# Two attention layers on one core: other PSUM banks and a split load at the start, and two kinds of VectorE work placed later

## The chip, the cores and the metric

The kernel runs on one core of a Trainium2 chip. A core has five engines that work side by side and wait for each other through semaphores: TensorE (matmuls, PE in the profile, with its weight loads as PEld), VectorE (DVE), ScalarE (ACT), GpSimd (POOL) and SyncE (SP), which issues most of the transfers. Matmuls write to PSUM, and VectorE or ScalarE must copy or add the result out of PSUM before a bank can be written again. The metric is the device time of one execution in microseconds (us). All data is float32.

## What is computed

Eight images of 32x32 positions and 256 channels go through two layers. The first is attention with four heads, an output projection and a residual; the second is attention with 32-channel queries and keys, scaled by gamma, with a residual.

```python
# layer 0; xf: (8, 1024, 256), 4 heads
qkv = einsum('bnc,cd->bnd', xf, W_qkv)             # per head q, k, v of 256 each
atten = softmax(einsum('bihd,bjhd->bijh', q, k) * 256**-0.5, axis=2)
res = einsum('bijh,bjhd->bihd', atten, v)
x = einsum('bnd,dc->bnc', res.reshape(B, -1, 1024), W_out) + b_out + xf
# layer 1
f, g, h = x @ Wf + bf, x @ Wg + bg, x @ Wh + bh     # f, g: 32 wide, h: 256 wide
b = softmax(einsum('bik,bjk->bij', g, f), axis=-1)
y = gamma * einsum('bij,bjd->bid', b, h) + x
```

## The kernel before

Positions are taken in two blocks of 512 (blk 0 and 1), channels in two halves of 128, since a tile has 128 partitions. In layer 0 the weights of a head are multiplied together first (`fold_weights`, lines 302 to 351): Wq with Wk transposed gives `wqk`, and Wv with that head's part of W_out gives `wvo`. For this the three weight blocks are turned by TensorE transposes against an identity (tasks `turn`, PSUM tiles pwq, pwk, pwv), copied to SBUF as wqT and wvT, and multiplied (tasks `multiply`, PSUM tiles pwqk and pwvo). `copy_on(i, dst, src)` puts a copy on VectorE where i is even and on ScalarE where it is odd.

Most products use Strassen's scheme with seven block products in place of eight (`seven`, line 235). Each has three PSUM banks, x, y and z, and is cut into three tasks, one, two and three. Task two ends with VectorE's `v = y + e` and `out22 = z + v`; task three's matmuls then write bank y again, so they wait for v. Operands of the block products are sums and differences of blocks, which VectorE makes beforehand: xs from the transposed image (`key_sums`), qs from the queries, ss from the exponentials of the scores, yt from the products.

PSUM has eight banks. The pool tagged "ps" holds six of them, for the scores and most block products; the pool "psm" holds two, for transposes, weight products and the output projection. Tiles of a pool go round: a new one starts when the reader of the one that many places back has finished.

For the first image the rows are turned by TensorE in `transpose_rows` (line 357, PSUM tiles px, copied to x0T by ScalarE). Later images are turned by small transfers on SP (`turn_rows`, line 401, issued at line 386) and VectorE's 32x32 transpose (line 394). The order at the start is written out (lines 965 to 971): turn q and k of head 0, half of px, multiply wqk, the rest of px, turn v, two of the xs sums, multiply wvo, the other two sums, then the first queries together with head 1's weights.

After that the program goes through steps (line 983 on), one for each head and block of layer 0 and one for each block of layer 1. For images 1 to 7 layer 1 of the image before comes between heads: after two heads, or after all four for the last image. In each step, tasks of several heads in flight are collected with a place on a scale of 0 to 10, and issued in the order of these places, to all engines. Scores of the step stand at 0, 2, 4, 6, 8 and 10 in layer 0; products and projections of the two steps before go between them. Each engine works through its own list in that order, so an instruction that waits holds up everything behind it on its engine.

Two kinds of tasks matter here besides the start.

- The scaling. The row sums of the exponentials are added over the partitions by POOL, go through DRAM to become a column, are inverted by VectorE (line 642), and go back through DRAM as a row that is broadcast to all partitions (`inv` and `invb`, lines 647 and 649, on SP's queue). One step after the projection, VectorE multiplies the projected tile `o` with it (line 700), and POOL issues a transfer that adds o to x1T, layer 1's input (line 703). The lists of these tasks are in `adds`.
- The next image's sums. While head 2 is worked on, the next image is turned, and in block 1 of that head its four xs sums are made (`key_sums`, line 433).

```python
        if i - 1 in adds:
            put(adds[i - 1], 0.5 if l0 or blk == 1 else 2.3)
...
            put(key_sums(a.b + 1), 0.5, 0.6, 6.4, 7.4)
```

Of the kernel before, what the change touches and what calls it, by code (L numbers as in the profile page):

```python
# [16 lines left out]
P = 128  # L17
# [3 lines left out]
def kernel(  # L21
# [52 lines left out]
    nc = tc.nc  # L74
    B, H, W, C = x.shape
# [5 lines left out]
    NB = 512  # L81
# [29 lines left out]
    def tile_of(tag, shape, name):  # L111
        return pools[tag].tile(shape, F32, tag=tag, name=name)


    rows, rows1 = {}, {}
# [57 lines left out]
    def copy_on(i, dst, src):  # L173
        if i % 2 == 0:
            nc.vector.tensor_copy(dst, src)
        else:
            nc.scalar.copy(dst, src)
# [6 lines left out]
    def load_weights(h, tag):  # L184

        nw = CC * 3 * C
        t = tile_of(tag, [P, nw + CC * C], f"w_{h}")
        w = t[:, :nw].rearrange("p (c d) -> p c d", c=CC)
        wo = t[:, nw:].rearrange("p (c d) -> p c d", c=CC)
        weights[h] = w, wo  # L190
        v = wqkv_v[:, :, ts(h, 3 * C)]

        def load_qk():
            nc.sync.dma_start(w[:, :, : 2 * C], v[:, :, : 2 * C])

        def load_v():
            nc.sync.dma_start(w[:, :, 2 * C :], v[:, :, 2 * C :])
            nc.sync.dma_start(wo, wout_v[:, ts(h, CC), :])

        return [load_qk, load_v]  # L200
# [4 lines left out]
    def sum_a(sums, a11, a12, a21, a22):  # L205
        tt = nc.vector.tensor_tensor
        s1, s2, s3, s4 = sums
        return [
            partial(tt, s1, a21, a22, ALU.add),
            partial(tt, s2, s1, a11, ALU.subtract),  # L210
            partial(tt, s3, a11, a21, ALU.subtract),
            partial(tt, s4, a12, s2, ALU.subtract),
        ]

    def sum_b(sums, b11, b12, b21, b22):
        tt = nc.vector.tensor_tensor
        t1, t2, t3, t4 = sums
        return [
            partial(tt, t3, b22, b12, ALU.subtract),
            partial(tt, t1, b12, b11, ALU.subtract),  # L220
            partial(tt, t2, b22, t1, ALU.subtract),
            partial(tt, t4, b21, t2, ALU.subtract),
        ]

    def a_operands(blocks, sums):
        a11, a12, a21, a22 = blocks
        s1, s2, s3, s4 = sums
        return dict(zip((1, 2, 3, 4, 5, 6, 7), (a11, a12, s4, a22, s1, s2, s3)))

    def b_operands(blocks, sums):  # L230
        b11, b12, b21, b22 = blocks
        t1, t2, t3, t4 = sums
        return dict(zip((1, 2, 3, 4, 5, 6, 7), (b11, b21, b22, t4, t1, t2, t3)))
# [65 lines left out]
    NARROW = dict(e="eh", u="uh", v="w")  # L299
    LAST = dict(e="eo", u="uo", v="w")  # L300

    def fold_weights(h):

        wT, hold = [], []
        folded[h] = []

        def turn(i, what):
            w, _ = weights[h]
            pt = tile_of("psm", [P, NB], f"pw{what}_{h}")
            for d in range(CC):  # L310
                for c in range(CC):
                    nc.tensor.transpose(
                        pt[:, d * C + c * P : d * C + (c + 1) * P],
                        w[:, c, i * C + d * P : i * C + (d + 1) * P],
                        ident,
                    )
            if i != 1:
                hold.append(tile_of("y", [P, N], f"w{what}T_{h}"))
            t = hold[-1][:, ts(i % 2, NB)]
            copy_on(i, t, pt)  # L320
            wT.append(t.rearrange("p (d c) -> p d c", d=CC))

        def multiply(i, what):
            pm = tile_of("psm", [P, NB], f"p{what}_{h}")
            for c in range(CC):
                for d in range(CC):
                    nc.tensor.matmul(
                        pm[:, ts(c, C)],
                        lhsT=wT[2 * i][:, d, ts(c, P)],
                        rhs=wT[1][:, d, :] if i == 0 else weights[h][1][:, d, :],  # L330
                        start=(d == 0),
                        stop=(d == CC - 1),
                    )
            t = const.tile([P, CC, C], F32, tag=f"{what}{h}", name=f"{what}{h}")
            copy_on(i, t.rearrange("p c e -> p (c e)"), pm)
            folded[h].append(t)
            if i == 0:
                t4 = const.tile([P, 4, P], F32, tag=f"wt{h}", name=f"wt{h}")
                sums = [t4[:, k, :] for k in range(4)]
                blocks = [t[:, c, ts(e, P)] for c in range(CC) for e in range(CC)]  # L340
                run(sum_b(sums, *blocks))
                wblocks[h] = b_operands(blocks, sums)
            else:
                t4 = const.tile([P, 4, P], F32, tag=f"wo{h}", name=f"wo{h}")
                sums = [t4[:, k, :] for k in range(4)]
                blocks = [t[:, c, ts(e, P)] for e in range(CC) for c in range(CC)]
                run(sum_a(sums, *blocks))
                oblocks[h] = a_operands(blocks, sums)

        tasks = [partial(turn, i, what) for i, what in enumerate(("q", "k", "v"))]  # L350
        tasks += [partial(multiply, i, what) for i, what in enumerate(("wqk", "wvo"))]
        return tasks


    xT_of, x1T_of, xblocks, vblocks = {}, {}, {}, {}

    def transpose_rows(b, src, dst, layer):


        def task(k, c):  # L360
            if b not in dst:
                dst[b] = tile_of("xT", [P, CC, N], f"x{layer}T_{b}")
            pt = tile_of("psm", [P, NB], f"px{layer}_{b}_{k}_{c}")
            for t in range(HT):
                nc.tensor.transpose(
                    pt[:, ts(t, P)], src[b][:, k * HT + t, ts(c, P)], ident
                )
            nc.scalar.copy(dst[b][:, c, ts(k, NB)], pt)

        return [partial(task, k, c) for k in range(NBLK) for c in range(CC)]  # L370
# [50 lines left out]
    def key_sums(b):  # L421

        made = {}

        def piece(i):
            if i == 0:
                xT = xT_of[b]
                t = tile_of("v", [P, 4, HN], f"xs_{b}")
                sums = [t[:, k, :] for k in range(4)]
                blocks = [xT[:, c, ts(k, HN)] for k in range(2) for c in range(CC)]  # L430
                made["l"] = sum_a(sums, *blocks)
                xblocks[b] = a_operands(blocks, sums)
            made["l"][i]()

        return [partial(piece, i) for i in range(4)]
# [479 lines left out]
    def run(*lists):  # L915
        for l in lists:
            for t in l:
                t()
# [27 lines left out]
    pm = tile_of("psm", [P, NB], "pm_idle")  # L946
# [10 lines left out]
    steps, adds = [], {}  # L957
# [6 lines left out]

    first = steps[0][0]
    queries, qsums = first.queries(), first.query_sums(0)
    turn_q, turn_k, turn_v, fold_qk, fold_vo = fold_weights(0)
    turn_x, sums = transpose_rows(0, rows, xT_of, 0), key_sums(0)
    fold = [fold_weights(h) for h in range(1, HEADS)]
    run([turn_q, turn_k], turn_x[:2], [fold_qk], turn_x[2:], [turn_v], sums[:2], [fold_vo])  # L970
    run(sums[2:], queries[:2], fold[0][:2], queries[2:], qsums)
    first_sums = value_sums(0)

    def is_l0(s):
        return s is not None and isinstance(s[0], Layer0)

    def step(k):
        return steps[k] if 0 <= k < len(steps) else None
# [4 lines left out]
    for i, (a, blk) in enumerate(steps):  # L983
        l0 = isinstance(a, Layer0)
        one, two, nxt = step(i - 1), step(i - 2), step(i + 1)
        places = []

        def put(tasks, *at):
            assert len(tasks) == len(at)
            places.extend(zip(at, range(len(places), len(places) + len(at)), tasks))  # L990
# [3 lines left out]
        else:  # L994
            tasks, _ = a.scores(blk)
            put(tasks, *((0.5, 2.4) if blk == 0 else (0.5, 2)))
        if is_l0(two):
            u, k = two
# [9 lines left out]
            if nxt is None:  # L1008
                put(adds[i], 4.2)
        if i - 1 in adds:  # L1010
            put(adds[i - 1], 0.5 if l0 or blk == 1 else 2.3)
        if is_l0(one):
            u, k = one
            sums, keys = u.sums(k)
# [31 lines left out]
        if l0 and a.h == 2 and a.b + 1 < B:  # L1046
            if blk == 0:
                put(moves[4:], 0.5, 1.5, 2.5, 3.5)
                put(turned, 6.4, 7.4, 8.4, 9.4)
            else:  # L1050
                put(key_sums(a.b + 1), 0.5, 0.6, 6.4, 7.4)

        if l0 and a.b > 0 and a.h == behind(a.b) - 1:
            if blk == 0:
# [106 lines left out]
    with tc.If(bad > 0), ExitStack() as general:  # L1161
# [7 lines left out]
        for b in range(B):  # L1169
# [3 lines left out]
            for h in range(HEADS):  # L1173
                a = General0(b, h, bout_sb)
# [4 lines left out]
            a = Layer1(b)  # L1179
# [37 lines left out]
```

## Time and profile before

| | |
|---|---|
| median of three runs | 2309.2 us (2309.19 to 2309.86) |
| profiled execution, whole | 2311.76 us |
| profiled execution, span of the program's instructions | 2309.9 us |
| TensorE granted clock | 1.00 |
| VectorE / ScalarE / POOL busy | 72% / 25% / 14% of the span |
| DMA, mean | 41 GB/s, 94.16 MB |

The span runs from the first instruction to the end of the last one. The profiled execution is a single one, and its own total is set beside its span. In the timeline a line has the start in us, the busy time in us, the engine, the source line, the operation, output and inputs by the program's names with their shapes, and how many instructions were merged; in brackets stands how long the engine was idle before it and who released it. Names without numbers stand for many tiles: psx, psy and psz are the three banks of any block product of the scores, and psy_y, psy_q and psy_o those of products, queries and projections.

### The profile page before, as it was taken

How to read it: one execution, taken by the hardware profiler on the slowest of the kernel's cores; microseconds unless marked ns; L12 is line 12 of the kernel's file. 1: busy time of each engine (PE TensorE's matmuls, PEld its weight loads, DVE VectorE, ACT ScalarE, POOL GpSimd, SP SyncE). 2: the span in 40 equal slices, each digit the busy share in tenths (PEclk: the TensorE clock that was granted, in tenths of full speed). 3: DMA queues.
4: the chain of work that ended last, by engine and by line, in shares of the span. 5: the costliest groups of instructions: out<-in, count | busy, mean ns of one | idle time of the engine just before them, and what ended most of it. 6: DMA issues, size and time to landing. Idle time of an engine off the chain costs nothing.

```text
span 2309.9 us, 27289 instructions
## 1 busy us (share of the span) xinstructions
PE 2299.7 (100%) x10256; PEld 1891.9 (82%) x10256; DVE 1663.3 (72%) x2963; ACT 585.5 (25%) x1015; POOL 317.9 (14%) x199
## 2 busy tenths in 40 slices
PE   9999999999999999999999999999999999999999
PEld 7888888788878888778887888878888788888887
DVE  7787787577875777657776677766777667777765
ACT  2222222222221222212232122221222222222223
POOL 0111112011120112101121011210112101111210
PEclk9999999999999999999999999999999999999999
DMA  4211123301233013220132201322113211121222
GB/s 137 33 28 26 21 38 52 74 15 28 35 52 68 15 28 47 47 61 15 28 55 43 58 15 28 58 42 55 19 23 58 42 37 19 28 45 25 40 45 49
DMA packets 239740, 94.16 MB, mean 41 GB/s; under 512 B 204208, under 2 KB 208944, under 8 KB 239600
## 3 DMA queue, kind: packets, MB, share of 16 engines
q1 hardware_dynamic: 220400, 55.10, 12.3%
q0 software_dynamic: 19200, 37.23, 9.2%
q8 instruction: 83, 1.36, 0.4%
q14 instruction: 57, 0.47, 0.1%
HBM read 29.76 MB, written 8.65 MB: 17 GB/s over the span
## 4 chain that ended last, share of the span: by engine, by line
PE 96%; DMA 3%; DVE 1%; SPq 0%; ACT 0%; issue 0%; DVEq 0%
PE psy_y L255 14%; PE psy L255 14%; PE psx_y L255 10%; PE psz_y L255 10%; PE psz L255 9%; PE psx L255 9%; PE pa_l L900 8%; PE psy_o L255 6%; PE psy_q L255 3%; PE pr_v_l L494 3%; PE psx_q L255 2%; PE psx_o L255 2%; PE psz_q L255 2%; DMA inv<-inverse 2%; PE ps_l L812 1%; DMA invb<-inv 1%
## 5 line engine op out<-in xcount | busy, mean ns | idle before, releaser
L626 POOL PARTITION_ALL_REDUCE rb<-rs x64 | 206.6, 3229 | 1429.2 <-DVE rs L624 901.3
L255 PE MATMUL psx<-q,x0T 128*128 128x256 f32 x1024 | 263.5, 380 | 0.0
L255 PE MATMUL psy<-qs,xs 128*128 128x256 f32 x1024 | 262.9, 379 | 0.0
L255 PE MATMUL psz<-q,xs 128*128 128x256 f32 x1024 | 262.8, 379 | 0.0
L576 ACT ACTIVATE p<-p 128x1024 f32<-128x1024 f32 x128 | 135.3, 1057 | 497.7 <-DVE p L272 497.7
L255 PE MATMUL psx_y<-p,x 128*128 128x256 f32 x1024 | 241.9, 379 | 0.0
L255 PE MATMUL psy_y<-p,xt 128*128 128x256 f32 x1024 | 241.9, 379 | 0.0
L900 PE MATMUL pa_l<-v_l,s_l 128*128 128x257 f32 x1024 | 231.5, 381 | 0.0
L255 PEld LDWEIGHTS psx<-q,x0T 128*128 128x128 f32 x1024 | 193.8, 190 | 45.3 <-issue 20.7
L255 PEld LDWEIGHTS psx_y<-p,x 128*128 128x128 f32 x1024 | 194.6, 190 | 34.1 <-issue 8.6
L900 PEld LDWEIGHTS pa_l<-v_l,s_l 128*128 128x128 f32 x1024 | 193.9, 190 | 32.9 <-issue 6.1
L255 PEld LDWEIGHTS psy<-qs,xs 128*128 128x128 f32 x1024 | 194.5, 190 | 26.8 <-DVE q L272 0.4
L255 PEld LDWEIGHTS psz<-q,xs 128*128 128x128 f32 x1024 | 194.6, 190 | 26.5
L255 PEld LDWEIGHTS psy_y<-p,xt 128*128 128x128 f32 x1024 | 194.6, 190 | 26.5
L284 ACT ACTIVATE p<-psx 128x512 f32<-128x512 f32 x128 | 76.4, 597 | 363.7 <-PE psx L255 363.5
L272 DVE TENSOR_TENSOR u<-psy,e 128x512 f32<-128x512 f32 x128 | 88.1, 689 | 87.0 <-ACT e L278 75.6
L703 POOL DMA_DIRECT2D x1T<-o x64 | 78.0, 1219 | 431.9 <-DVE o L700 303.6
L255 PE MATMUL psy<-qs,x0T 128*128 128x256 f32 x512 | 132.6, 381 | 1.6 <-DVE v L272 1.6
L272 DVE TENSOR_TENSOR v<-psy,e 128x512 f32<-128x512 f32 x128 | 88.3, 690 | 53.0 <-PE psy L255 51.7
L255 PE MATMUL psy_y<-ss,xt 128*128 128x256 f32 x512 | 121.4, 380 | 0.1
L255 PE MATMUL psz_y<-ss,xt 128*128 128x256 f32 x512 | 120.9, 379 | 0.0
L255 PE MATMUL psz_y<-ss,x 128*128 128x256 f32 x512 | 120.9, 379 | 0.0
(141 smaller groups left out, 3419.4 us busy)
## 6 DMA issues: line engine op xcount, KB each, us to landing
x1T<-o POOLq DMA_DIRECT2D x64, 512.0 KB, 5.0
invb<-inv SPq DMA_DIRECT2D x63, 256.0 KB
x<-x1T SPq DMA_DIRECT2D x256, 32.0 KB
out_dram<-x SPq DMA_DIRECT2D x15, 512.0 KB
x<-in_x_dram SPq DMA_DIRECT2D x14, 512.0 KB
x0T<-x SPq DMA_DIRECT2D x224, 32.0 KB
fg<-v_l POOLq DMA_DIRECT2D x56, 64.0 KB, 2.1
w<-in_L_conv_W_qkv_dram SPq DMA_DIRECT2D x4, 512.0 KB
```

Of the source, the lines that this page charges most:

```text
L255: nc.tensor.matmul(banks[k][:, ts(i, w)], lhsT=lhsT, rhs=rhs, start=first and n == 0, stop=True, skip_group_check=True,)
L272: nc.vector.tensor_tensor(dst, shaped(banks[k]), shaped(other), ALU.add)
L284: copy(outs["11"](), shaped(banks["x"]))
L494: nc.tensor.matmul(pm[:, ts(j, C)], lhsT=src()[:, c, ts(2 * t2 + j, P)], rhs=w()[:, c, :], start=(c == 0), stop=(c == CC - 1),)
L576: exp(both, both)
L626: nc.gpsimd.partition_all_reduce(t, r.rearrange("p e i -> p (e i)"), P, bass_isa.ReduceOp.add)
L703: nc.gpsimd.dma_start(x1T_of[self.b][:, :, ts(blk, NB)], o, accum_op=ALU.add)
L812: nc.tensor.matmul(pm, lhsT=self.f[ts(r, CK), ts(j0 + r, P)], rhs=self.g[ts(r, CK), ts(blk, NB)], start=True, stop=True,)
L900: nc.tensor.matmul(pm[:, : C + 1], lhsT=p[:, j, ts(ti, P)], rhs=v[:, j, : C + 1], start=(j == 0), stop=(j == NT - 1),)
```

## The change

- The first load of head 0's weights, q and k in one transfer of 512 KB, becomes two transfers of 256 KB, one for q and one for k. Other heads keep one transfer.
- The transposes and weight products of head 0 and the transposes of the first image's rows take their PSUM tiles from "ps" in place of "psm" (nine tiles).
- In all four heads the copy of the turned v weights (wvT) moves from VectorE to ScalarE: `(i + 1) // 2` is 0 for q, 1 for k and 1 for v. The copies of wqT, wqk, wkT and wvo stay.
- The scaling moves from place 0.5 to place 2.3 in the first layer-0 step after layer 1 (six steps, images 1 to 6). In all other steps it keeps its place.
- In block 1 of head 2, the second and fourth of the next image's four sums move from 0.6 to 4.3 and from 7.4 to 9.2.

The order of instructions on TensorE, POOL and, but for the split load, SP is the same in both kernels. On VectorE and ScalarE only the pieces named here change their places.

```diff
         def load_qk():
-            nc.sync.dma_start(w[:, :, : 2 * C], v[:, :, : 2 * C])
+            for i in range(2 if h == 0 else 1):
+                d = ts(i, C) if h == 0 else slice(0, 2 * C)
+                nc.sync.dma_start(w[:, :, d], v[:, :, d])
...
-    def fold_weights(h):
+    def fold_weights(h, tag="psm"):
...
-            pt = tile_of("psm", [P, NB], f"pw{what}_{h}")
+            pt = tile_of(tag, [P, NB], f"pw{what}_{h}")
...
-            copy_on(i, t, pt)
+            copy_on((i + 1) // 2, t, pt)
...
-            pm = tile_of("psm", [P, NB], f"p{what}_{h}")
+            pm = tile_of(tag, [P, NB], f"p{what}_{h}")
...
-    def transpose_rows(b, src, dst, layer):
+    def transpose_rows(b, src, dst, layer, tag="psm"):
...
-            pt = tile_of("psm", [P, NB], f"px{layer}_{b}_{k}_{c}")
+            pt = tile_of(tag, [P, NB], f"px{layer}_{b}_{k}_{c}")
...
-    turn_q, turn_k, turn_v, fold_qk, fold_vo = fold_weights(0)
-    turn_x, sums = transpose_rows(0, rows, xT_of, 0), key_sums(0)
+    turn_q, turn_k, turn_v, fold_qk, fold_vo = fold_weights(0, "ps")
+    turn_x, sums = transpose_rows(0, rows, xT_of, 0, "ps"), key_sums(0)
...
         if i - 1 in adds:
-            put(adds[i - 1], 0.5 if l0 or blk == 1 else 2.3)
+            put(adds[i - 1], 0.5 if is_l0(one) == l0 else 2.3)
...
             else:
-                put(key_sums(a.b + 1), 0.5, 0.6, 6.4, 7.4)
+                put(key_sums(a.b + 1), 0.5, 4.3, 6.4, 9.2)
```

## The prediction

> **What bounds the kernel now.** I read the page's engine table first, then its chain of work, then the timeline wherever the start of one matmul stands further from the start of the one before than the same form needs elsewhere.
>
> ```profile
> PE 2299.7 (100%) x10256; PEld 1891.9 (82%) x10256; DVE 1663.3 (72%) x2963; ACT 585.5 (25%) x1015; POOL 317.9 (14%) x199
> PE 96%; DMA 3%; DVE 1%; SPq 0%; ACT 0%; issue 0%; DVEq 0%
> 4.78 0.63 PE L312 MATMUL pwq<-ident,w 128*128 128x128 f32 x4 [0.23 <-DMA w<-in_L_conv_W_qkv_dram]
> 6.19 1.09 PE L365 MATMUL px<-ident,x 128*128 128x128 f32 x8 [0.35 <-DVE wqT L175]
> 7.53 1.99 PE L327 MATMUL pwqk<-wqT 128*128 128x256 f32 x8 [0.24 <-ACT x0T L368]
> 10.30 0.66 PE L365 MATMUL px<-ident,x 128*128 128x128 f32 x4 [0.35 <-DVE wqk L175]
> 11.43 0.69 DVE L175 COPY wvT<-pwv 128x512 f32<-128x512 f32 x1
> 12.23 1.97 PE L327 MATMUL pwvo<-w,wvT 128*128 128x256 f32 x8 [0.83 <-ACT x0T L368]
> ...
> 432.46 1.23 DVE L700 TENSOR_TENSOR o<-o,invb 128x1024 f32<-128x1024 f32 x1 [3.68 <-DMA invb<-inv]
> 433.61 0.68 DVE L272 TENSOR_TENSOR v<-psy,e 128x512 f32<-128x512 f32 x1
> 434.35 1.13 PE L255 MATMUL psy<-qs,x0T 128*128 128x256 f32 x4 [0.30 <-DVE v L272]
> ...
> 458.50 0.69 DVE L433 TENSOR_TENSOR xs<-xs,x0T 128x512 f32<-128x512 f32 x1
> 459.71 0.69 DVE L272 TENSOR_TENSOR v<-psy,e 128x512 f32<-128x512 f32 x1 [0.52 <-PE psy L255]
> 464.87 1.97 PE L255 MATMUL psy_y<-ss,xt 128*128 128x256 f32 x8
> ...
> 476.10 0.68 DVE L433 TENSOR_TENSOR xs<-x0T,xs 128x512 f32<-128x512 f32 x1
> 476.70 0.68 DVE L620 TENSOR_TENSOR rs<-rs,ss 128x512 f32<-128x512 f32 x1
> 477.30 0.68 DVE L272 TENSOR_TENSOR v<-psy,e 128x512 f32<-128x512 f32 x1
> 478.04 1.13 PE L255 MATMUL psy<-qs,x0T 128*128 128x256 f32 x4
> ```
>
> TensorE is the bound: it is busy all but about 10 us of a span of 2309.9 us, so no part can gain more than the few places where it stands still. Steady starts are 0.216 us apart for a 256-column matmul, 0.43 for 512 columns and 0.109 for a transpose. Three kinds of gap touch this change. (1) In the first 12.3 us TensorE waits in turn for a load, for PSUM copies and for wvT. (2) In the first layer-0 step after layer 1, VectorE holds the scaling (L700) until the broadcast invb has landed, and v, which TensorE needs next, stands behind it. (3) In the step of head 2, block 1, two TensorE starts come late, at 464.87 and 478.04; the same two recur in images 1 to 6.
>
> **What the Trainium skill says.** "Perfetto Trace Analysis", section "Tensor Engine Instruction (MATMUL, LD_WEIGHTS)", says that a matmul's end is estimated and that VectorE and ScalarE take their work strictly in order. The trace agrees: busy shows nearly no idle where starts still reveal gaps, and v waits behind L700 although its PSUM input was ready. "PSUM — Partial Sum Buffer", section "Specifications (TRN2)", gives 8 banks of 512 fp32: here 6 are tag ps and 2 psm, one 128x512 tile each, so a pool of two lets a third tile start only when the first is copied (6.19 above). "DMA: Bandwidth & Descriptors", section "Issuing engines are not separate DMA queues", says that all transfers share 16 engines. The trace agrees: from 3 us on they are full at 318 to 408 GB/s, so a split load cannot bring later data sooner.
>
> **Part 1: the start.** TensorE's instruction order stays as it was; only banks, one copy's engine and the first load change. Before: the trace records the last completion of q and k together at 4.65 us, of x's four pieces at 5.33, 5.99, 7.57 and 8.21, of v at 8.92. Work starts 0.13 after (4.65 to 4.78). After: q alone is half the bytes, so pwq can begin as soon as the idle matmuls end, about 4.4; k lands as before, or up to 0.3 later, since a 1 KB packet takes 46 ns where 2 KB took 84[...]. I take 0.1 for this and for every load behind it; SP issues one more DMA (0.45 us), hidden because the engines are full and not SP. So pwk starts at 4.9 (before 5.25). px no longer waits for the wqT copy, but its third transpose needs x's second piece: 5.99+0.1+0.13 = 6.22, two transposes later 6.44, the second px to 6.88, and pwqk starts then instead of at 7.53. It takes 8 x 0.216; the third px starts at 8.61, the fourth at 9.05 with no wait for wqk, pwv at 9.48 (x complete 8.4, v 9.2, both in time). A copy starts 0.63 after the first of four transposes (9.36 to 9.99), and ScalarE starts the next 0.52 later (33.91 to 34.43). So ScalarE copies at 9.24, 9.76 and, with wvT now behind them, 10.28 to 10.87. pwvo starts 0.11 later, 10.98, against 12.23: 1.25 gained, of which I book 1.2. Everything after hangs on pwvo (wvo copy, wo sums, xs, u_q, psy_q at 17.73) and moves with it. Bounds: 0.7 if the loads come 0.5 later, 1.4 if not at all. The three other wvT copies (0.6 each) go to ScalarE, busy 25%. The one in a tight place falls after the exponentials at 33.91 and puts e about 0.7 later, u about 0.3; the matmul that needs u is at 38.5, so nothing is paid. VectorE loses 4 copies of 0.68 there, but at 31.05 and 64.11 it waits for wvo and wqk, not for wvT: no gain.
>
> **Part 2: the scaling.** It moves from 0.5 to 2.3 in six steps, behind v and its p. Excess at TensorE's start over the steady spacing, with the 0.10 by which the second matmul then lags: 0.57 (434.35), 0.14 (718), 0.76 (1003), 0.00 (1287), 0.70 (1572), 0.34 (1856); sum 2.5 us. After: v needs psy (its matmuls start at 429.55, plus 0.86 and 0.2), so it runs at 430.6, 3 us sooner; TensorE wants it at 433.9. L700 still starts at 432.46 when invb lands, so the DMA that POOL issues is no later. Behind L700 now stand the reciprocal of pa (ready 434.1) and the sums; L700 ends at 433.7, before them. What I cannot see is how far these waits exist without the profiler: the profiled run took 2311.76, 1.9 of it outside the span, against a median of 2309.2, and a landing only 0.7 us earlier leaves none. Bounds 0 to 2.5; I take 2.5, because the landing is behind small x0T transfers on SP's queue which belong to the program.
>
> **Part 3: the next image's sums.** The second piece moves from 0.6 to 4.3. At 459.71 v waits for TensorE and not for it, so the gap at 464.87, which comes from v, p, ss, v_q, q, ss in a row, stays; between 467 and 469.4 VectorE has 1.8 us free for the 0.68. The fourth moves from 7.4 to 9.2. VectorE has no pause from 469.5 to 478, so rs, v and p come 0.6 sooner: v is done at 477.4, before TensorE is ready at 477.88. Gain 0.16+0.10 = 0.26, times 6 = 1.6 us. At 9.2 it fills the same 0.6 before p<-psy (479.75), so p, its exponentials and the next e keep their times; the next matmul that needs u is at 486.8, over 3 us after it. Image 0 shows no gap, and has room for both. Bounds 0 to 1.6, or 3.1 if the gap at 464.87 goes too.
>
> **Sum.** 1.2 + 2.5 + 1.6 = 5.3 us in the profiled execution: 2309.9 to 2304.6 of span. Taken off the median: 2303.9, say 2304.0 us, 0.23% faster. The line between faster and no change is drawn at 0.2% (4.6 us), about what a measurement of this kernel can tell from no change.
>
> **Rivals.** A: the waits for invb hardly occur without the profiler. For it: the profiled run is 2.5 us longer than the median, the size of part 2; against: no row ties that difference to these waits. Time 2309.2-2.8 = 2306.4. B: loads, not banks, hold the start, and part 1 gives 0.3. For it: x's second piece would be px's limit; against: the later gain at 12.23 doesn't hang on x. 2309.2-4.4 = 2304.8. C: the gap at 464.87 goes as well, since VectorE's queue is lighter. Against it is the 0.52 of idle before v: 2302.4. D, slower: L700, now in front of the reciprocals and both remaining sums of its group, waits for an invb that lands much later. The sums' bank is next written at 441.4, with some 2.5 us of VectorE work (L700, reciprocal, sum) to do first, so it costs only from a landing near 438, 5.5 us later than now; past it each us costs 6 us in all. A landing 7 us later gives 2309.2-2.8+9 = 2315.4. For it: the inv transfer took 9 to 11 us; against: invb landed 2.8 to 3.9 us after u in all six images, and nothing is added ahead of it. E: the change does not do what it says: the comparison of instruction orders excludes that for the moved pieces; the banks follow from the tags.
>
> **Numbers.** Forecast 0.50, A 0.27, B 0.05, C 0.12, D 0.06. Faster by over 0.2% is forecast and C, 0.62; within it A and B, 0.32; slower D, 0.06. The range 2302.4 to 2306.9 runs from C to A with the low bound of part 1, and leaves out D and part of the tails.
>
> **What would show it.** pwvo near 11 us; no start over 0.05 us late in the L1-to-L0 steps; starts at 464.87's place unchanged and at 478.04's on time; L700 after p. A pwvo still past 11.8, or a new start late behind L700 or xs, would make the forecast wrong.

## The result, and the profile after

The changed kernel takes 2313.32 us (median of 20 runs, 2312.69 to 2315.31) against 2309.82 us of the kernel before (20 runs beside it, 2309.19 to 2311.16). The ratio is 1.0016, 95% interval 1.001 to 1.0022. It is slower by 3.5 us, where 5.2 us less had been forecast.

The profiled executions differ less: spans of 2311.3 and 2309.9 us, so +1.4. The execution of before that was profiled was itself 1.9 us above the median of those 20 runs. That matters below, since what it spent there had been booked as a gain.

The engine table and the chain of waits after:

```profile
span 2311.3 us, 27291 instructions
...
PE 2299.4 (99%) x10256; PEld 1893.2 (82%) x10256; DVE 1671.5 (72%) x2959; ACT 587.4 (25%) x1019; POOL 317.8 (14%) x199
...
PE 96%; DVE 3%; issue 0%; DMA 0%; ACT 0%; SPq 0%; DVEq 0%
```

TensorE is still the bound. But VectorE's busy time rose by 8.2 us although it has four copies of 0.68 fewer, and the chain now runs over VectorE for 3% of the span where it was 1%. Some VectorE instruction has become longer. The view of waits on TensorE (who was waited for, total us, number of times, longest) shows where that is paid:

```profile
PE psz L257 <- DVE p L274: 3.3, 6, 0.5
...
PE px L367 <- DMA x<-in_x_dram: 1.0, 2, 0.7
PE pwvo L329 <- ACT wvT L177: 0.8, 1, 0.8
```

Six waits of psz for p are new, one for each of images 1 to 6. The timeline of after at the first of them, in the step of head 2, block 1:

```profile
476.91 0.68 DVE L274 TENSOR_TENSOR v<-psy,e 128x512 f32<-128x512 f32 x1
...
478.09 1.03 PE L257 MATMUL psy<-qs,x0T 128*128 128x256 f32 x4
...
478.82 3.23 POOL L628 PARTITION_ALL_REDUCE rb<-rs  x1 [43.15 <-issue]
...
479.36 2.24 DVE L435 TENSOR_TENSOR xs<-x0T,xs 128x512 f32<-128x512 f32 x1
481.52 0.68 DVE L274 TENSOR_TENSOR p<-psy,e 128x512 f32<-128x512 f32 x1
482.12 0.68 DVE L274 TENSOR_TENSOR p<-psz,u 128x512 f32<-128x512 f32 x1
482.25 1.13 PE L257 MATMUL psz<-q,xs 128*128 128x256 f32 x4 [0.55 <-DVE p L274]
```

Two things are to be seen. The wanted part works: v runs at 476.91 and psy starts at 478.09 on time, without the lag of before. But the fourth sum, which always took 0.68 us, takes 2.24 at its new place, where POOL's all-reduce has begun 0.54 us ahead of it. p<-psy comes 1.77 us later than before (481.52, was 479.75), and the psz matmuls start 0.06 after its end, at 482.25 where the steady spacing gives 481.54: 0.71 late, and 0.10 more by which the next matmul lags. The psz matmuls of the kernel before had some 1.1 us of slack behind that p (p<-psy ended at 480.43, psz started at 481.60).

The groups of the fourth sum (nanoseconds: least, median, most of eight), before and then after:

```profile
L433 DVE TENSOR_TENSOR xs<-x0T,xs x8: 683/684/685, 16.4 to 1897.8; 128x512 f32<-128x512 f32 x8
```

```profile
L435 DVE TENSOR_TENSOR xs<-x0T,xs x8: 683/2236/2237, 16.9 to 1901.8; 128x512 f32<-128x512 f32 x8
```

Only the one made in the start phase, with no all-reduce near, kept its 0.68. Against this stand the other differences of the two traces: start +0.48 (psy_q at 18.21, was 17.73), the scaling's waits -2.47, the six late starts at 478.04's place -1.57, the six new ones +4.88 (0.81 each), one of 0.29 in image 0. The sum is +1.6, measured +1.4.

The start after, TensorE alone:

```profile
4.64 1.06 PE L314 MATMUL pwq<-ident,w 128*128 128x128 f32 x4
5.49 1.06 PE L314 MATMUL pwk<-ident,w 128*128 128x128 f32 x4
6.83 0.44 PE L367 MATMUL px<-ident,x 128*128 128x128 f32 x2 [0.27 <-DMA x<-in_x_dram]
7.99 0.87 PE L367 MATMUL px<-ident,x 128*128 128x128 f32 x6 [0.72 <-DMA x<-in_x_dram]
8.70 1.89 PE L329 MATMUL pwqk<-wqT 128*128 128x256 f32 x8
...
12.68 1.99 PE L329 MATMUL pwvo<-w,wvT 128*128 128x256 f32 x8 [0.78 <-ACT wvT L177]
```

The waits for PSUM copies are gone and a longer wait for x has come. x's second piece is complete at 7.94 us by the trace's last completion; before it was 5.99, although the same bytes, q, k and x's first piece, stand ahead of it. The windows (us, busy of PE, PEld, DVE, ACT, POOL, then the granted clock, DMA share, GB/s), before and then after:

```profile
4.00:5.00 1.00, 0.77 (x6) 0.61 (x6) 0.00 (x0) 0.00 (x0) 0.00 (x0) 1.00 1.06 408
5.00:6.00 1.00, 0.85 (x8) 0.61 (x6) 0.55 (x1) 0.12 (x1) 0.00 (x0) 1.00 1.06 318
```

```profile
4.00:5.00 1.00, 1.00 (x6) 1.00 (x6) 0.00 (x0) 0.00 (x0) 0.00 (x0) 1.00 0.78 203
5.00:6.00 1.00, 1.00 (x7) 1.00 (x6) 0.26 (x1) 0.00 (x0) 0.00 (x0) 1.00 0.58 184
```

The engines that had been full at 408 and 318 GB/s now move 203 and 184, 0.78 and 0.58 busy, in the two microseconds in which x's first pieces come in.

The scaling after, VectorE in the first step behind layer 1:

```profile
431.39 0.69 DVE L274 TENSOR_TENSOR v<-psy,e 128x512 f32<-128x512 f32 x1 [1.83 <-PE psy L257]
432.12 0.69 DVE L274 TENSOR_TENSOR p<-psz,v 128x512 f32<-128x512 f32 x1
432.73 1.22 DVE L702 TENSOR_TENSOR o<-o,invb 128x1024 f32<-128x1024 f32 x1
```

v waits for TensorE alone, L702 comes behind p, and no TensorE start is late there in any of the six places.

### The profile page after: what moved, and what is told of

It is laid out like the page before. It is cut to its first block, busy times and chain, and to the rows that moved or that the text cites. A ratio compares the mean times of both kernels' runs of the same rounds, so it can differ in the third digit from the quotient of the medians.

```text
span 2311.3 us, 27291 instructions
## 1 busy us (share of the span) xinstructions
PE 2299.4 (99%) x10256; PEld 1893.2 (82%) x10256; DVE 1671.5 (72%) x2959; ACT 587.4 (25%) x1019; POOL 317.8 (14%) x199
## 4 chain that ended last, share of the span: by engine, by line
PE 96%; DVE 3%; issue 0%; DMA 0%; ACT 0%; SPq 0%; DVEq 0%
PE psy_y L257 14%; PE psy L257 14%; PE pa_l L902 10%; PE psz_y L257 10%; PE psz L257 9%; PE psx L257 9%; PE psx_y L257 9%; PE psy_o L257 6%; PE psy_q L257 4%; PE pr_v_l L496 3%; PE psx_o L257 2%; PE psx_q L257 2%; PE psz_q L257 2%; PE ps_l L814 1%; DVE xs L435 1%; PE pm_fg L769 1%
```

## The experiments

Kernels sent together ran on one chip with the kernel before between them, and a ratio is against those runs. The median of before differed between the chips: 2311.55 us beside e1 to e4, 2310.20 beside e5 to e8, 2309.53 beside e9 and e10. Times of different groups are therefore compared by their ratios. Theory P in the expectations says that the fourth sum is blocked by POOL's all-reduce; Q explains the late psz without it.

**e1: the changed kernel with the sums at their old places.**

```diff
-                put(key_sums(a.b + 1), 0.5, 4.3, 6.4, 9.2)
+                put(key_sums(a.b + 1), 0.5, 0.6, 6.4, 7.4)
```

> The changed kernel with the next image's four sums at their old places (0.5, 0.6, 6.4, 7.4). Theory P (the fourth sum, at 9.2, runs beside POOL's all-reduce, takes 2.24 us in place of 0.68, and with it the last sum of p and the next group's z matmul come 0.8 us late in six images) and theory Q (any VectorE work put there makes z late) both expect the starts near 482 to be on time, the gap of 0.26 us at v near 478 back, and 2313.3 - 4.9 - 0.3 + 1.6 = about 2309.7 us. Theory R (the later loads at the start are most of the loss) expects about 2313.

Measured: 2309.41 us, ratio 0.9991 (0.9982 to 1.0). None of the six new late starts is left, and the small ones of 0.26 at 478.04's place are back. So the loss is in the sums' places, and without them the change is no slower than before. That the time itself came so near the 2309.7 expected is partly luck: before ran at 2311.55 us on this chip and not at 2309.8, so against it this kernel gained 2.1 us where 0.1 had been worked out. The times of e2 and e3 below meet their 2308.1 in the same way; what decides there are the traces.

**e2 and e3: only the fourth sum moves, once ahead of the last rs addition, which releases POOL, and once behind p.**

```diff
-                put(key_sums(a.b + 1), 0.5, 4.3, 6.4, 9.2)
+                put(key_sums(a.b + 1), 0.5, 4.3, 6.4, 8.6)     # e2
+                put(key_sums(a.b + 1), 0.5, 4.3, 6.4, 10.2)    # e3
```

> The changed kernel with the fourth sum at 8.6, so ahead of the last addition of rs (8.7) that starts POOL's all-reduce; the same 0.68 us of VectorE work still stands ahead of the last two sums of p. P: the sum takes 0.68 us in all seven images, z near 481.5 starts less than 0.1 us late, no gap near 478, about 2313.3 - 4.9 - 0.3 = 2308.1 us. Q: z stays 0.2 to 0.7 us late in each of six images, 2310 to 2313 us.

> The changed kernel with the fourth sum at 10.2, behind both last sums of p but still while POOL's all-reduce runs. P: the sum still takes 1.2 us or more, since POOL has not ended, but nothing on TensorE waits for it, about 2308.1 us. Q: the sum takes 0.68 us there, and the time is the same 2308.1 us; the length of the sum tells the two apart.

Measured: e2 2308.23 us, ratio 0.9989 (0.998 to 0.9998); e3 2308.09 us, ratio 0.9988 (0.9979 to 0.9997). Neither has a late TensorE start near 478 or 482. The timelines of e2 and then of e3:

```profile
478.25 0.68 DVE L435 TENSOR_TENSOR xs<-x0T,xs 128x512 f32<-128x512 f32 x1
...
479.44 3.23 POOL L628 PARTITION_ALL_REDUCE rb<-rs  x1 [43.03 <-issue]
...
479.98 0.68 DVE L274 TENSOR_TENSOR p<-psy,e 128x512 f32<-128x512 f32 x1
```

```profile
478.31 3.23 POOL L628 PARTITION_ALL_REDUCE rb<-rs  x1 [42.92 <-issue]
...
478.85 0.68 DVE L274 TENSOR_TENSOR p<-psy,e 128x512 f32<-128x512 f32 x1
...
480.12 0.97 DVE L435 TENSOR_TENSOR xs<-x0T,xs 128x512 f32<-128x512 f32 x1
```

In e2 the sum stands in the same queue, ahead of the same p, done before POOL starts: it takes 0.68 and costs nothing. So it is not one more instruction ahead of p that hurts. In e3 p, which reads one operand from PSUM, keeps its 0.68 beside the all-reduce, while the sum behind it, with both operands in SBUF, is stretched. P holds and Q falls. The stretch in e3 was only 0.29 us, less than P had said, and that gives the mechanism its size. In the changed kernel the sum starts 0.54 us after POOL and ends 2.78 after it; less its own 0.68 that is 2.10. In e3 it is 1.81 + 0.97 - 0.68 = 2.10. It looks as if such an instruction can begin only 2.10 us after the all-reduce began, wherever in that time it came. In e3's image 0 it came 2.33 us after POOL's start, and took 0.68.

**e4: the kernel before with the new places of the sums alone.**

```diff
-                put(key_sums(a.b + 1), 0.5, 0.6, 6.4, 7.4)
+                put(key_sums(a.b + 1), 0.5, 4.3, 6.4, 9.2)
```

> The kernel before with the four sums at the new places alone (0.5, 4.3, 6.4, 9.2). P and Q: 2309.8 + 4.9 + 0.3 - 1.6 = about 2313.4 us, seven late z starts. R: within 1 us of before, 2309.8, since start and scaling are those of before.

Measured: 2315.15 us, ratio 1.0017 (1.0009 to 1.0024), +3.6 us. That is as large as the whole loss of the change, in the kernel before. Its timeline has the same lines:

```profile
480.05 2.24 DVE L433 TENSOR_TENSOR xs<-x0T,xs 128x512 f32<-128x512 f32 x1
482.20 0.68 DVE L272 TENSOR_TENSOR p<-psy,e 128x512 f32<-128x512 f32 x1
482.94 1.13 PE L255 MATMUL psz<-q,xs 128*128 128x256 f32 x4 [0.55 <-DVE p L272]
```

The six psz starts of images 1 to 6 are 0.70 to 0.71 late, as after; a seventh, in image 0, is 0.41 late.

**e5: the kernel before with the scaling's new place alone.**

```diff
-            put(adds[i - 1], 0.5 if l0 or blk == 1 else 2.3)
+            put(adds[i - 1], 0.5 if is_l0(one) == l0 else 2.3)
```

> The kernel before with the scaling alone moved to 2.3 in the six steps. Theory S (the waits at v behind L700 are as the profile of before shows them, 2.5 us in all) expects 2.5 us less than before, ratio 0.9989. Theory A (they hardly occur in most runs, and the profiled run of before had more of them than its median) expects 0.3 to 1 us less. In both, no start of psy late near 434, 1003, 1572 and 1856 us.

Measured: 2309.81 us, ratio 0.9998 (0.999 to 1.0006). In its trace v waits for no scaling anywhere, so the move does what it says. It is worth 0.4 us, not to be told from nothing. How much there is to gain differs from execution to execution: the trace shown of before had 2.5 us of these waits in all; e4's, with the scaling at its old place, has four late starts of 0.05 to 0.19, and at the old place too e6's has one of 0.33, e7's two of 0.54 and 0.20, e8's one of 0.13 (each without the 0.10 of the lag behind it). With the lags that is 0.3 to 1.0 us in each of these four traces.

**e6, e7 and e8: the start. All of it (e6), banks and copy without the split load (e7), the split load alone (e8), each in the kernel before.** e6 takes the hunks of the change up to and including the banks of head 0; e7 leaves out the first of them, shown here; e8 has only that one.

```diff
-            nc.sync.dma_start(w[:, :, : 2 * C], v[:, :, : 2 * C])
+            for i in range(2 if h == 0 else 1):
+                d = ts(i, C) if h == 0 else slice(0, 2 * C)
+                nc.sync.dma_start(w[:, :, d], v[:, :, d])
```

> The kernel before with the start alone changed (banks, wvT on ScalarE, q and k in two loads). Theory L (x's second piece now lands so late that the freed banks bring nothing) expects pwvo at 12.4 to 13 us and a time within 0.5 us of before. The recorded forecast's theory (banks hold the start) expects pwvo near 11 us and 1.2 us less.

> The start of the changed kernel with q and k in one load again. If the split is what makes x late, x's second piece lands near 6.0 us, pwqk starts near 6.9, pwvo near 11 and the time is 1.2 us under before. If x's landing varies from run to run whatever the loads, pwvo comes between 11 and 13 and the time within 0.5 us of the start with the split.

> The kernel before with the split load alone. If the split makes x late (last piece of the first block after 7.5 us), px ends late and pwvo starts at 12.8 to 13.5, about 0.7 us slower than before. If not, pwvo stays at 12.2 to 12.9 and the time is that of before.

Measured: e6 2310.32 us, ratio 1.0001 (0.9993 to 1.0009); e7 2309.09, ratio 0.9994 (0.9986 to 1.0002), 1.1 us less than before; e8 2310.91, ratio 1.0003 (0.9995 to 1.0011), 0.7 more. Each interval holds 1, so the order e7, e6, e8 isn't shown by the times alone and rests on the traces as well. TensorE in e7:

```profile
6.68 1.20 PE L365 MATMUL px<-ident,x 128*128 128x128 f32 x8
7.72 1.89 PE L327 MATMUL pwqk<-wqT 128*128 128x256 f32 x8
...
11.70 1.56 PE L327 MATMUL pwvo<-w,wvT 128*128 128x256 f32 x6 [0.78 <-ACT wvT L177]
```

Without the split px runs through its eight transposes without a pause, since x's second piece is complete at 6.13, and pwvo starts at 11.70, against 12.23 in the trace of before and 12.82 in that of e5, which has the start of before. With the split that piece came at 7.95 in e6 and 7.75 in e8, and pwvo at 12.69 and 14.86. In e8's trace TensorE also ran pwqk at half its rate, and that execution took 1.2 us more than e8's median, so its 14.86 can't be put down to the split alone.

**e9: without the split, with the scaling's new place, and with the second pair of sums at 4.3 and 4.4, far from the all-reduce. e10: the same, but the first load cut in two by rows, so that its packets keep their 2 KB.** Both from the changed kernel:

```diff
-                d = ts(i, C) if h == 0 else slice(0, 2 * C)
-                nc.sync.dma_start(w[:, :, d], v[:, :, d])
+                r = slice(i, i + 1) if h == 0 else slice(0, CC)          # e10; e9: one load
+                nc.sync.dma_start(w[:, r, : 2 * C], v[:, r, : 2 * C])
...
-                put(key_sums(a.b + 1), 0.5, 4.3, 6.4, 9.2)
+                put(key_sums(a.b + 1), 0.5, 0.6, 4.3, 4.4)
```

> The changed kernel with q and k loaded in one transfer again and the four sums of the next image at 0.5, 0.6, 4.3 and 4.4 (so neither the second nor the fourth stands where it meets POOL's all-reduce, and both are gone before the tight place near 477). Theory P (the fourth sum lost the time, the split costs about 0.7 to 1.2 us, banks and the ScalarE copy gain about 1.1): no late start near 477.5 or 481.5, first pwvo near 11.7, time 2.5 to 3.5 us below the kernel before (ratio 0.9985 to 0.9989). If the split is free: pwvo near 11.7 all the same, but no gain over e2 and e3, ratio 0.9989 to 0.9992. If an xs sum at 4.3 meets something else on VectorE: a new late start between 467 and 470 in images 1 to 6, ratio above 0.999.

> As e9, but the first load is again cut in two transfers of 256 KB, this time by the input channels (each transfer has both q and k of one half of the rows, so its packets stay 2 KB), where the change cut it by columns into packets of 1 KB. Theory S (the size of the first packets delays the transfers behind them): x's second piece lands near 6.1 us as without the split. Theory T (one more transfer at the head of the queues delays what is behind it, whatever its packets): x's second piece lands near 7.5 to 8 us and pwvo starts near 12.5. Time: S as e9 within 0.3 us, T 0.7 to 1.2 us over e9.

Measured: e9 2306.58 us (21 runs, 2305.95 to 2307.39), ratio 0.9987 (0.9981 to 0.9994): 3.0 us below the kernel before, and faster than both kernels. e10 2307.71 us (12 runs, 2306.62 to 2307.96), ratio 0.9991 (0.9983 to 1.0), 1.1 us over e9 on the same chip. TensorE's waits in e9 and then in e10:

```profile
PE pwvo L327 <- ACT wvT L177: 0.8, 1, 0.8
PE psy L255 <- DVE v L272: 0.3, 1, 0.3
...
```

```profile
PE px L367 <- DMA x<-in_x_dram: 1.0, 1, 1.0
PE pwvo L329 <- ACT wvT L177: 0.8, 1, 0.8
...
```

The wait of psy in e9, at 30 us, is found in all twelve traces. In e9 no transpose waits for a load and pwvo starts at 11.16, sooner than the 11.7 expected (its first load is complete at 4.56, e7's at 4.81). In e10 x's second piece is complete at 7.77, though every packet is of 2 KB. Packet size is not the cause (S of e10 falls); one more transfer at the head of the queue is enough (T). What the split costs is shown by this pair and not by e9 against e2 and e3, which keep the split: their ratios, 0.9987, 0.9989 and 0.9988, can't be told apart. In all six traces with a split load beside the one shown of after (e1, e2, e3, e6, e8, e10) that piece came at 7.66 to 8.27 us; in the five without (before, e4, e5, e7, e9) at 5.91 to 6.36. From 4 to 6 us the DMA engines move 194 to 259 GB/s in the seven traces with a split load, 0.68 to 0.92 busy, and 327 to 363 GB/s, full, in the five without; why stays open. What the traces show is that the fourth transfer of SP's list is complete at 7.57 to 8.27 in all twelve, whether it is x's second piece or its third: only what that piece holds has changed.

## Why the prediction was wrong

The failed step is in part 3: "At 9.2 it fills the same 0.6 before p<-psy (479.75), so p, its exponentials and the next e keep their times". The fourth sum was costed at its duration elsewhere, 0.68. At that place it takes 2.24, because the rs addition that releases POOL stands three instructions ahead of it, and POOL has begun when it comes. The path was short of a step too: the prediction looked for what waits behind this p at the matmul that needs u (486.8), and not at the psz matmuls at 481.60, whose 1.1 us of slack the p that came 1.77 later used up. The term "0 to 1.6, or 3.1" had no bound on the side of a loss; it measured +3.6 us alone (e4). By the trace's own terms: -1.57 for the starts at 478.04's place, as predicted; +4.88 for six new late starts of 0.71 and 0.10; +0.29 in image 0.

The trace of before had the evidence. The scaling L700 reads o and invb, both in SBUF. Alone it takes 1.22; where it meets an all-reduce, seven times, it looks like this in the kernel before:

```profile
401.40 3.22 POOL L626 PARTITION_ALL_REDUCE rb<-rs  x1 [15.99 <-issue]
...
401.81 2.90 DVE L700 TENSOR_TENSOR o<-o,invb 128x1024 f32<-128x1024 f32 x1
```

0.41 + 2.90 - 1.22 = 2.09: the same time as for the sum. The least, median and most of this operation's durations, side by side, would have shown it. "SBUF — State Buffer" of the Trainium skill, section "Who interferes with whom", says it as a rule: a VectorE instruction with two SBUF inputs contends with a GpSimd instruction that reads SBUF, one with at most one SBUF input doesn't (outside some modes, which operations on two tensors don't have). The runs agree on both halves: 2.24 for 0.68 and 2.90 for 1.22, while p, v_y and y, with a PSUM operand each, keep 0.68 and 0.42 beside the all-reduce. Its section "🔬 SBUF: two separate sides" calls the shared ports a lock that is held for the whole instruction. Here the second comer goes on 2.10 us after the start of an all-reduce whose record is 3.23 long; the measurement decides, though a span on POOL is rough, and its reads may be over by then.

The other steps, one by one:

- Part 1, 1.2 gained: wrong, 0.1 lost (e6), by two opposite terms. Banks and ScalarE copy gain 1.1 (e7, an interval that holds 1), near what was booked. The split was booked at 0.1 for all loads behind it and took that gain away again: 1.1 in e10 against e9, and 0.7 alone (e8, not to be told from nothing). What failed there is the reason given, that the 16 engines are full: with the split they were 0.58 to 0.78 busy from 4 to 6 us. The bound of "0.7 if the loads come 0.5 later" didn't reach far enough, since x's second piece came 1.85 later than taken (7.94 for 6.09). Rival B had the place right, x's second piece as px's limit, but took it as a limit that stays and not as one that the split brings. The start of pwq at 4.4 was missed too (4.64, behind the idle matmuls), and its transposes ran 0.21 apart instead of 0.109. "TensorE: Matmul & The Clock Gate", section "What's actually happening", describes an array clock that is halved until some microseconds of work have passed. The spacing fits that, though the windows show a granted clock of 1.00 there, so the cause isn't shown. With px waiting for x until 7.99 it cost nothing here.
- Part 2, 2.5 gained: the mechanism was right (v, then L702, no late start), the size wrong. 0.4 (e5), since the profiled execution of before had more of these waits than most. The doubt had been put into words as rival A. Its reason, that the profiled execution was longer than the median (by 2.5 us then, by 1.9 with all 20 runs), was the better one. One difference stays open: on the chip of e1, where before ran longer, start and scaling together gave 2.1 (with an interval that reaches to nothing), on the other chip, apart, 0.3; e4's trace, from the first of these chips, has no more than 1.0 us of scaling waits, lags included, to explain it.
- The second sum at 4.3: right, it takes 0.68 at 467.18 in a pause of VectorE, and the start at 464.87's place stays 0.26 late. Rival C didn't come.
- D, the one slower rival, had the wrong instruction: L702 is not late. E is excluded by the traces.

On medians the parts alone give +3.6 (e4) - 0.4 (e5) + 0.1 (e6) = +3.3, and the whole measured +3.5. That this comes out so near is no proof of the smaller terms: with e1's -2.1 in place of e5 and e6 the sum is +1.5. Only the sums' term is clear of noise by itself.

## What to carry to other kernels

Before moving a VectorE instruction, ask what runs on GpSimd at its new place, and whether both its inputs lie in SBUF; look up whether the same operation has two durations in the trace already, and what stood beside the long ones. A wait that one profiled execution shows is a gain only as far as the other runs have it too, and an execution above its own median warns of it. A load that is cut so that its first half comes sooner can put a later one off: look at the arrival of all that follow.

## What the hardware showed that was not expected

- VectorE instructions with both inputs in SBUF (the xs sums and the scaling), started during a 3.23 us all-reduce on GpSimd, ended 2.10 us plus their own duration after the all-reduce's start. Every one that came inside the 2.10 us, in each of the twelve traces, gives 2.09 to 2.10; the one that came at 2.33 was not delayed.
- Cutting the first 512 KB load in two, by columns or by rows, brought its halves in sooner (the first complete at 3.45 to 3.87 us instead of 4.56 to 5.09 for the whole), and the third and fourth transfer didn't gain: the fourth ended at 7.66 to 8.27 with the cut and 7.57 to 8.09 without, with 256 KB less moved.
